# A two-layer spectral kernel on one core: the first transform as a written list over two chunks and three matrices, with weights prepared beside it

## The chip, the core and the metric

The kernel runs on one core of a Trainium2 chip. The metric is the device time of one execution in microseconds. The engines are named as the profile names them: PE (matrix multiplication; PEld is its loading of weights), DVE (vector engine), ACT (scalar engine), POOL (GpSimd) and SP, whose queue issues all DMAs of this kernel.

## The reference

`x` is [4, 256, 256, 64] in float32: batch, rows h, columns w, channels. Layer 0 works on each image, layer 1 along the rows for each channel.

```python
# layer 0
h  = layernorm(x) @ w_te + b_te                        # 64 -> 128 channels
F  = fft2(h, axes=(1, 2))
fc = gelu(concat(real(F), imag(F)) @ w_fc + b_fc)
sp = real(ifft2(fc[..., :128] + 1j * fc[..., 128:], axes=(1, 2)))
x1 = x + sp @ w_tp + b_tp
d  = gelu(depthwise_conv3x3(layernorm(x1) @ w_fe + b_fe))
x2 = x1 + d @ w_fp + b_fp
# layer 1: a moving average over 25 rows, the rest filtered per channel
trend = moving_average(x2, 25)
xs = rfft(x2 - trend, axis=1)[:, :128]
ys = einsum('bmnc,cmk->bknc', xs, w_real + 1j * w_imag)
out = trend + irfft(ys padded, n=256, axis=1)
```

## The kernel before

All sums are in float32. Because the first linear step commutes with the transform, the transform is taken over the 64 input channels, and `w_te` is folded into `w_fc` (`wp`). Layer 1 is linear per channel, so for each of the 64 channels the kernel builds one 256x256 matrix (average, transform, weights and inverse together), stores it in DRAM (`m_d`), and at the end multiplies by it.

The stages of one execution are:

- **Preparation** of the weights in the pool `prep` (lines 193 to 308): some twenty small loads, then `centre`, `w_teg`, `wp`, `w_feg`, the taps `w_dwh`, twenty-four products into `wc_main` and `wc_half`, and the edge terms. It stands ahead of everything else in program order. The pool `prep` is closed before the pool `fwd` of the first transform is opened in the same memory.
- **The first transform**, `forward_h`, in 32 chunks for each image. A chunk `j` is loaded into `xt` (`fl`, lines 371 to 379, three buffers). ACT squares it (`fq`, line 328, one buffer); DVE sums it (`fr`, line 331), sums the squares (`fm`, line 338), and forms the variance (`fR` and `fM`, lines 335 and 342); POOL takes the inverse root (`fp`, line 348) and scales the chunk (`fx`, line 355); DVE forms half sums into `xb`, of which there is one buffer (`fa`, line 392), and quarter sums back into `xt` (`fb`, line 412); POOL forms the sum and the difference of the two row halves (`fh0` and `fh1`, line 417), again into `xb`; PE transforms (`y0` and `y1`, line 423); ACT evicts (`yt0` and `yt1`, line 441), and SP stores to `y_d` (line 454).
- **Layer 1's matrices**, `matrices`: for each channel, `first` on PE and its copy on ACT (lines 1091, 1092 and 1094), `second` on PE (line 1101), `third` on DVE (line 1112) and a store to `m_d` (line 1113). Weights come four channels at a time (line 1087).
- **The spectrum**, `spectral`: groups of columns are read back from `y_d` into `yb` (line 483); the special first column is split into `yr` (line 500); then transform along w (`x`, line 528, and `xs`), the mixing product (`m0`, `m1`, line 552), copies, sums and differences (`gc`, `b`, line 571), GELU (`g`, line 575), a fold on POOL (`p`, line 581), projection (`z`, line 605), a turn (`w`, line 622), and the way back along w (`u` to `uf`, lines 654 to 716).
- **The convolution** and the end of layer 0, then layer 1's products (`layer1`, line 1163).

The four engines PE, DVE, ACT and POOL execute their instructions in program order. Program order is written out by hand: `period(n)` walks a list of names with offsets (`SPECTRUM` while only the first transform and the spectrum run, `FULL` when the convolution runs too), and `do(op, index)` first emits whatever `FOLLOWS` says must come earlier. Ahead of the periods stand S0 = 35 calls of `starting(n, m)`. Each treats one chunk and two matrices, so the first transform of image 0 (32 chunks and three of the next image) and all 64 matrices end together. Then `load_group(0)` and `begin(0)` open the spectrum, and `period(n)` follows from n = 35. The queue of SP is filled by a scheduler. PSUM has eight banks of 128 x 512, handed out in turn.

Of the kernel before, what the change touches and what calls it, by code (L numbers as in the profile page):

```python
# [20 lines left out]
C = 64  # L21
# [108 lines left out]
def conv_seq_kernel(ctx: ExitStack, tc: tile.TileContext, a: dict, tables: bass.AP, out: bass.AP):  # L130
# [29 lines left out]
    nc.sync.dma_start(tab, tables[:, :_L0_END])  # L160
# [31 lines left out]

    with tc.tile_pool(name="prep", bufs=1) as prep:

        def load(shape, name, src):
            t = prep.tile(shape, F32, tag=name, name=name)
            nc.sync.dma_start(t, src)
            return t

        w_te = load([C, HID], "w_te", a["w_te"])  # L200
        g1 = load([C, 1], "g1", column(a["g1"]))
        b1 = load([C, 1], "b1", column(a["b1"]))
        b_te = load([HID, 1], "b_te", column(a["b_te"]))
        nc.sync.dma_start(w_fc, a["w_fc"].rearrange("(k p) n -> p k n", p=P))
        with nc.allow_non_contiguous_dma(reason="a few weights, once"):
            nc.sync.dma_start(b_fc, a["b_fc"].rearrange("(k p) -> p k", p=P))
        nc.sync.dma_start(w_tp, a["w_tp"])
        nc.sync.dma_start(b_tp, row(a["b_tp"]))
        nc.sync.dma_start(w_fp, a["w_fp"])

        centre = prep.tile([P, P], F32, tag="centre", name="centre")
        nc.vector.tensor_scalar(centre, ident, float(C) ** 0.5, None, ALU.mult)
        for lo in (0, C):
            dst = centre[lo : lo + C, lo : lo + C]
            nc.vector.tensor_scalar(dst, dst, -(float(C) ** -0.5), None, ALU.add)


        w_teg = prep.tile([C, HID], F32, tag="w_teg", name="w_teg")  # L220
        nc.vector.tensor_scalar(w_teg, w_te, g1, None, ALU.mult)
        ps = bank("ps_teT")
        nc.tensor.matmul(ps[:, :C], w_teg, centre[:C, :C], start=True, stop=True)
        w_tegT = prep.tile([HID, C], F32, tag="w_tegT", name="w_tegT")
        nc.vector.tensor_copy(w_tegT, ps[:, :C])
        ps = bank("ps_wp")
        for k in range(2):
            nc.tensor.matmul(
                ps[k * C : (k + 1) * C, : 2 * HID], w_tegT, w_fc[:, k, :], start=True, stop=True
            )  # L230
        nc.vector.tensor_copy(wp, ps[:, : 2 * HID])

        ps = bank("ps_dc")
        nc.tensor.matmul(ps[:, 0:1], w_te, b1, start=True, stop=True)
        nc.vector.tensor_scalar(v_dc, ps[:, 0:1], b_te, NPOS, ALU.add, ALU.mult)
        nc.vector.tensor_scalar(nw_tp, w_tp, -1.0, None, ALU.mult)
        nc.vector.tensor_scalar(b_tp, b_tp, 2.0 * NPOS, None, ALU.mult)
        nc.vector.memset(at_dc, 1.0)


        w_fe = prep.tile([P, HID], F32, tag="w_fe", name="w_fe")
        g2 = prep.tile([P, 1], F32, tag="g2", name="g2")
        for par in range(2):
            nc.sync.dma_start(w_fe[par * C : (par + 1) * C], a["w_fe"])
            nc.sync.dma_start(g2[par * C : (par + 1) * C], column(a["g2"]))
        b2 = load([C, 1], "b2", column(a["b2"]))
        b_fe = load([HID, 1], "b_fe", column(a["b_fe"]))
        b_dw = load([HID, 1], "b_dw", column(a["b_dw"]))
        taps = a["w_dw"].rearrange("y x i o -> (y x i) o")
        w_dw = load([9, HID], "w_dw", taps)  # L250
        w_dwb = load(
            [P, 9, HID], "w_dwb", row(taps.rearrange("k o -> (k o)")).to_broadcast([P, 9 * HID])
        )
        b_fe9 = load([9, HID], "b_fe9", row(a["b_fe"]).to_broadcast([9, HID]))
        w_feg = prep.tile([P, HID], F32, tag="w_feg", name="w_feg")
        nc.vector.tensor_scalar(w_feg, w_fe, g2, None, ALU.mult)
        ps = bank("ps_feg")
        nc.tensor.matmul(ps[:, :HID], centre, w_feg, start=True, stop=True)
        nc.vector.tensor_copy(w_feg, ps[:, :HID])


        w_dwh = prep.tile([P, 3, 4, HID], F32, tag="w_dwh", name="w_dwh")
        tap = lambda dy: w_dwb.rearrange("p (y x) o -> p y x o", x=3)[:, dy]
        nc.vector.tensor_copy(w_dwh[:, :, 0], tap(0))
        nc.vector.tensor_copy(w_dwh[:, :, 3], tap(2))
        w_mid = prep.tile([P, 3, HID], F32, tag="w_mid", name="w_mid")
        w_sum = prep.tile([P, 3, HID], F32, tag="w_sum", name="w_sum")
        nc.vector.tensor_scalar(w_mid, tap(1), 0.5, None, ALU.mult)
        nc.vector.tensor_tensor(w_sum, tap(0), tap(2), ALU.add)
        for k, op in ((1, ALU.add), (2, ALU.subtract)):  # L270
            nc.vector.scalar_tensor_tensor(w_dwh[:, :, k], w_sum, 0.5, w_mid, ALU.mult, op)
        for dst, lo, dx in (
            (wc_main[0:C, 0], 0, 1),
            (wc_main[C:P, 0], C, 2),
            (wc_main[0:C, 1], 0, 0),
            (wc_main[C:P, 1], C, 1),
            (wc_half[0:C], 0, 2),
            (wc_half[C:P], C, 0),
        ):
            for k in range(4):  # L280
                nc.vector.tensor_tensor(
                    dst[:, k], w_feg[lo : lo + C], w_dwh[lo : lo + C, dx, k], ALU.mult
                )

        ps = bank("ps_b9")
        nc.tensor.matmul(
            ps[0:9, :HID], b2.to_broadcast([C, 9]), w_fe[0:C], start=True, stop=True
        )
        b9 = prep.tile([9, HID], F32, tag="b9", name="b9")
        nc.vector.tensor_tensor(b9, b_fe9, ps[0:9, :HID], ALU.add)  # L290
        r_edge = prep.tile([9, HID], F32, tag="r_edge", name="r_edge")
        nc.vector.scalar_tensor_tensor(r_edge, b9, -1.0, w_dw, ALU.mult, ALU.mult)
        edge = load([9, 2 * N + 8], "edge", tables[0:9, _L0_END:_L1_START])
        ps = bank("ps_ec")
        nc.tensor.matmul(ps, r_edge, edge[:, 0 : 2 * N], start=True, stop=True)
        nc.vector.tensor_copy(edge_cols.rearrange("p e n -> p (e n)"), ps)
        ps = bank("ps_er")
        nc.tensor.matmul(ps[:, 0:8], r_edge, edge[:, 2 * N :], start=True, stop=True)
        nc.vector.tensor_copy(edge_rows.rearrange("p j e -> p (j e)"), ps[:, 0:8])
        ps = bank("ps_w9")  # L300
        nc.tensor.transpose(ps[:, 0:9], w_dw, ident[0:9, 0:9])
        sum9 = prep.tile([P, 1], F32, tag="sum9", name="sum9")
# [50 lines left out]
    def scale(src, dst, rstd):  # L353
        n = src.shape[1]
        nc.gpsimd.tensor_tensor(dst, src, rstd.unsqueeze(2).to_broadcast([P, n, C]), ALU.mult)


    y_ds, u_ds = {}, {}

# [1006 lines left out]
```

## Time and profile before

| what | value |
|---|---|
| median of 4 executions | 4493.59 us (4487.2 to 4506.36) |
| the profiled execution's own time | 4492.93 us |
| its span | 4491.1 us |
| PE busy | 4357.1 us (97%) |
| DVE busy | 3547.8 us (79%) |
| POOL busy | 2803.4 us (62%) |
| ACT busy | 2505.5 us (56%) |
| first load of a chunk of x issued | 26.71 us after the start of the span |
| first matmul of the first transform | 46.61 us |
| first matmul of the spectrum | 342.34 us |

All views show one execution. A group in the list of costly groups has a busy time, a count and a mean duration; the timeline lists single instructions in order of time with their start and duration in us, and in brackets the idle time of the engine before them and what ended it. In the timeline, a 128x512 matmul in float32 is recorded as two instructions. The table by windows gives the busy time of each engine in a stretch of the span, the granted clock of PE (1.00 is full speed) and the busy share of the DMA engines.

### The profile page before, as it was taken

The numbers are of one execution on the slowest core, as the hardware profiler recorded it, in microseconds if no ns is written. First come the engines' busy times: TensorE is split into PE (matmuls) and PEld (weight loads), VectorE is DVE, ScalarE is ACT, GpSimd is POOL, SyncE is SP. The second block draws the span as 40 slices with busy tenths as digits, with TensorE's granted clock in tenths as the row PEclk, the third lists the DMA queues.
The fourth block names the chain that finished last, engine by engine and source line by source line (L and its number), as shares of the span: only waits on it lengthen the run. The fifth ranks groups of instructions, "written<-read, shape, count | busy, mean of one in ns | idle before, by whom it ended". The sixth has DMA issues, their size and how long they took to land.

```text
span 4491.1 us, 63495 instructions
## 1 busy us (share of the span) xinstructions
PE 4357.1 (97%) x22347; PEld 2220.6 (49%) x22347; DVE 3547.8 (79%) x5451; ACT 2505.5 (56%) x3686; POOL 2803.4 (62%) x1806
## 2 busy tenths in 40 slices
PE   7998999899999999999999999999999999999999
PEld 4553333345555555455555555555555455554444
DVE  6778999899999999999999777777777788862222
ACT  2337888666666666666666666666664334331111
POOL 5888999787777777877777555555554555530000
PEclk9999999999999999999999999999999999999999
DMA  5665555434444444444444343333334332329986
GB/s 172 202 192 162 150 152 153 133 103 135 135 134 135 134 128 141 122 132 132 132 132 118 104 113 94 108 100 95 106 106 142 113 98 90 104 82 336 331 327 257
DMA packets 756581, 655.00 MB, mean 146 GB/s; under 512 B 40141, under 2 KB 649375, under 8 KB 747944
## 3 DMA queue, kind: packets, MB, share of 16 engines
q1 hardware_dynamic: 756264, 650.95, 47.4%
q8 instruction: 178, 2.92, 0.3%
q14 instruction: 139, 1.14, 0.1%
HBM read 364.81 MB, written 286.00 MB: 145 GB/s over the span
## 4 chain that ended last, share of the span: by engine, by line
PE 80%; POOL 7%; DVE 4%; issue 4%; DMA 2%; ACT 1%; SPq 0%; POOLq 0%; DVEq 0%; ACTq 0%
PE ps_h_c L903 19%; PE ps_h_c L922 11%; PE ps_o L1163 9%; PE ps_p L552 8%; PE ps_f_c L978 5%; PE ps_z L605 5%; PE ps_s_c L820 5%; PE ps_u L654 4%; PE ps_x L528 4%; PE ps_y L423 3%; POOL xb L417 3%; PE ps_t_c L857 3%; PE ps_ft_c L999 3%; POOL rstd L348 2%; PE ps_zt L622 2%
## 5 line engine op out<-in xcount | busy, mean ns | idle before, releaser
L581 POOL TENSOR_TENSOR g<-g 128x512 f32<-128x512 f32 (+1 forms) x520 | 738.0, 1432 | 521.5 <-ACT g L575 521.4
L903 PE MATMUL ps_h_c<-td_c,wc_main 128*128 128x512 f32 x2048 | 921.7, 593 | 0.0
L571 DVE TENSOR_TENSOR g<-ps_p,g 128x512 f32<-128x512 f32 x1040 | 692.8, 682 | 32.4 <-ACT g L566 14.4
L575 ACT ACTIVATE g<-g,b_fc 128x1024 f32<-128x1024 f32 (+1 forms) x520 | 586.3, 1147 | 179.9 <-DVE g L571 177.5
L348 POOL TENSOR_TENSOR rstd_c<-var_c,minus_half 128x16 f32<-128x16 f32 x128 | 372.0, 2907 | 466.4 <-DVE var_c L342 456.9
L566 ACT COPY g<-ps_p 128x512 f32<-128x512 f32 (+1 forms) x520 | 302.3, 583 | 457.8 <-PE ps_p L552 439.8
L903 PEld LDWEIGHTS ps_h_c<-td_c,wc_main 128*128 128x128 f32 x2048 | 369.1, 190 | 369.8 <-issue 304.2
L552 PE MATMUL ps_p<-xs,wp 64*128 64x512 f32 (+1 forms) x2080 | 519.5, 604 | 32.7 <-ACT xs L543 32.7
L922 PEld LDWEIGHTS ps_h_c<-td_c,wc_half 64*128 64x128 f32 x4032 | 416.4, 187 | 243.4 <-issue 194.1
L922 PE MATMUL ps_h_c<-td_c,wc_half 64*128 64x128 f32 (+1 forms) x4032 | 514.6, 392 | 3.4 <-POOL td_c L877 3.4
L1163 PE MATMUL ps_o<-xc,mt 128*128 128x512 f32 x1024 | 445.0, 596 | 14.8 <-DMA xc<-x_d 14.8
L348 POOL TENSOR_TENSOR rstd<-var,minus_half 128x16 f32<-128x16 f32 x128 | 373.3, 2916 | 84.9 <-DVE var L342 50.5
L954 DVE TENSOR_TENSOR h_c<-h_c,ps_h_c 128x512 f32<-128x512 f32 x512 | 317.5, 683 | 125.3 <-PE ps_h_c L922 125.2
L971 ACT ACTIVATE h_c<-h_c,b_conv 128x1024 f32<-128x1024 f32 x256 | 280.7, 1145 | 201.3 <-DVE h_c L967 201.3
L1177 DVE TENSOR_SCALAR oc<-ps_o,b_fp 128x512 f32<-128x512 f32 x128 | 96.1, 751 | 361.5 <-PE ps_o L1163 361.5
L417 POOL TENSOR_TENSOR xb<-xt 128x512 f32<-128x512 f32 x256 | 324.5, 1290 | 90.4 <-DVE xt L412 86.0
L947 DVE TENSOR_TENSOR h_c<-h_c,ps_h_c 128x512 f32<-128x512 f32 x256 | 175.7, 686 | 198.6 <-PE ps_h_c L922 194.4
L1163 PEld LDWEIGHTS ps_o<-xc,mt 128*128 128x128 f32 x1024 | 195.0, 191 | 264.1 <-issue 238.4
L528 PEld LDWEIGHTS ps_x<-tab,yb 128*64 128x64 f32 x4064 | 243.1, 139 | 129.8 <-issue 91.5
L605 PE MATMUL ps_z<-g,w_tp 128*64 128x512 f32 x1024 | 281.0, 611 | 22.0 <-POOL g L581 20.5
L1175 ACT ACTIVATE oc<-ps_o,b_fp 128x512 f32<-128x512 f32 x128 | 88.0, 687 | 373.1 <-PE ps_o L1163 258.1
L552 PEld LDWEIGHTS ps_p<-xs,wp 64*128 64x128 f32 x2080 | 195.4, 187 | 194.4 <-issue 121.8
(137 smaller groups left out, 7725.3 us busy)
## 6 DMA issues: line engine op xcount, KB each, us to landing
y_d<-yt SPq DMA_DIRECT2D x256, 256.0 KB, 2.5
yb<-y_d SPq DMA_DIRECT2D x256, 256.0 KB, 3.4
x_c<-in_x_dram SPq DMA_DIRECT2D x128, 512.0 KB, 5.0
u_d<-ut SPq DMA_DIRECT2D x256, 256.0 KB, 4.0
x_d<-st SPq DMA_DIRECT2D x128, 512.0 KB, 4.7
xc<-x_d SPq DMA_DIRECT2D x64, 1024.0 KB, 7.5
out_dram<-oc SPq DMA_DIRECT2D x256, 256.0 KB, 3.1
xt<-in_x_dram SPq DMA_DIRECT2D x504, 128.0 KB, 2.5
```

Source lines behind the costliest of these rows:

```text
L348: nc.gpsimd.tensor_tensor(rstd, var, minus_half.to_broadcast([P, n]), ALU.pow)
L417: nc.gpsimd.tensor_tensor(sums[j][:, i], x0, x1, (ALU.add, ALU.subtract)[i])
L528: nc.tensor.matmul(ps[r * C : (r + 1) * C, j * N + t * P : j * N + (t + 1) * P], blk[:, t, k, r * C : (r + 1) * C], tb[:, t, :], start=Tru ...
L552: nc.tensor.matmul(ps[:, :nf], wp[rows, cols], rhs[rows], start=True, stop=r == 1 or not pr["special"],)
L571: nc.vector.tensor_tensor(gt[:, i], re, gt[:, 1], op)
L575: nc.scalar.activation(g, g, AF.Gelu, bias=b_fc[:, half : half + 1])
L581: nc.gpsimd.tensor_tensor(g[:, 0], g[:, 0], g[:, 1], op)
L605: nc.tensor.matmul(ps[r * C : (r + 1) * C, :nf], w_tp, d[:, :nf], start=True, stop=True)
L903: nc.tensor.matmul(ps, wc_main[:, par, k, :], ts[(*j, k)].rearrange("p j i -> p (j i)"), start=True, stop=False,)
L922: nc.tensor.matmul(pss[k, par][:, s * P : (s + n) * P], wc_half[lo : lo + C, k, :], ts[(*at_q, k)][lo : lo + C, at : at + n, :].rearrange( ...
L954: nc.vector.tensor_tensor(g, g, m, (ALU.add, ALU.subtract)[r])
L1163: nc.tensor.matmul(ps[:, :nf], mts[i // CM][:, i % CM, t, to * P : (to + 1) * P], xc[:, t, :, :, i, :], start=t == 0, stop=t == 1,)
```

## The change

- The preparation becomes a generator, `prepare(prep)`: its loads come first, and its arithmetic is cut into pieces at thirty-two `yield`s, single products of `wc_main` and `wc_half` among them. Two pieces are taken in each call of `starting` from n = 1 on. `prep` gets memory of its own beside `matrices`, on the side of the convolution. The loads of chunk 0, of layer 1's tables and first weights, and of chunk 1 stand ahead of the loads of `tab` and of the weights.
- `starting(n, prep)` now treats two chunks and three matrices, in the order of the list `FIRST`, and is called 17 times. This covers 34 chunks and 51 matrices.
- For the chunks of image 0 (`j < 32`) the difference `fh1` is formed on DVE; the sum `fh0` stays on POOL.
- A matrix is now four names, `v`, `vc`, `mm` and `mt`, which a list can place.
- Between the first transform and the spectrum, four more matrices and the steps of chunk 34 are emitted after `load_group(0)` and ahead of `begin(0)` (`BETWEEN`).
- The last nine matrices go beside the spectrum: the first eleven periods (n = 35 to 45) follow the list `SPECTRUM_AND_MATRIX`. The convolution's pool is opened after them.

The later periods follow the same lists as before. `statistics` and `scale` only move in the file.

```diff
+        yield            # (in prepare: after the loads, and between pieces of the arithmetic)
...
             for k in range(4):
+                yield
                 nc.vector.tensor_tensor(
                     dst[:, k], w_feg[lo : lo + C], w_dwh[lo : lo + C, dx, k], ALU.mult
                 )
...
-            nc.gpsimd.tensor_tensor(sums[j][:, i], x0, x1, (ALU.add, ALU.subtract)[i])
+            engine = nc.vector if i and j < P // 4 else nc.gpsimd
+            engine.tensor_tensor(sums[j][:, i], x0, x1, (ALU.add, ALU.subtract)[i])
...
         def first(c):
-            ps = bank(f"ps_v_{c}")
...
+            if c % CG == 0 and c + CG < C:
+                load(c + CG)
+            ps = pss[c] = bank(f"ps_v_{c}")
...
+        load(0)
+        return {"v": first, "vc": between, "mm": second, "mt": third}
...
+    FIRST = numbered("""
+        v mm:-4 mt:-4 mm:-2 y1:-2 fq fl:1 vc fr yt1:-2 y0:-2 fm fR mm fM v:1 fq:1 fa:-1 v:2 fb:-1 fp
+        fh1:-1 fm:1 fh0:-1 mt:-2 yt0:-2 fr:1 y1:-1 fR:1 y0:-1 fx mt fM:1 fa fb fp:1 fh0 fl:2 fh1
+        fx:1 vc:2 vc:1 yt0:-1 yt1:-1
+    """)
+    SPECTRUM_AND_MATRIX = numbered("""
+        x:1 fq g1:-1 x z:-2 xs:1 zs:-2 v xs fl:1 p1:-1 w:-2 vc b0:-1 fr fm zt:-2 g0:-1 p0:-1 m0 m1
+        gc1 y1:-2 u b1 z:-1 gc0 fx:-1 b0 zs:-1 y0:-2 fR g1 w:-1 us fM yt1:-2 fa:-1 g0 mm:-1 m1:1 uc
+        p1 m0:1 fb:-1 yt0:-2 gc1:1 b1:1 gc0:1 p0 fh1:-1 mt:-1 fp uf fh0:-1 zt:-1
+    """)
...
+    BETWEEN = [
+        numbered("fl:1 fq fr fR"), numbered("fm fM fp"), numbered("fa:-1 fb:-1 fh0:-1 fh1:-1"),
+        numbered("fx y0:-2 y1:-2 yt0:-2 yt1:-2"),
+    ]
+    AHEAD = len(BETWEEN)
+    BESIDE = C - 3 * (S0 // 2) - AHEAD
...
-    def starting(n, m):
-
-        products, add = m
-        rows = lambda text, n: [do(op, n) for op in text.split()]
-        rows("fq", n)
-        rows("fl", n + 1)
-        rows("fr fR fm fM fp", n)
-        rows("fa fb", n - 1)
-        add()
-        products(2 * n)
-        add()
-        if n + 1 < S0:
-            rows("fx", n)
-        rows("y0 y1 yt0 yt1", n - 2)
-        rows("fh0 fh1", n - 1)
-        products(2 * n + 1)
+    def starting(n, prep):
+
+        for i, (op, at) in enumerate(FIRST):
+            do(op, (3 if op in MATRICES else 2) * n + at)
+            if n and i % (len(FIRST) // 2) == 0:
+                next(prep, None)
...
-                for n in range(S0):
-                    starting(n, m)
-                m[1]()
+                do("fl", 1)
+                nc.sync.dma_start(tab, tables[:, :_L0_END])
+                pieces = prepare(prep)
+                next(pieces)
+                nc.sync.dma_start(b_fp, row(a["b_fp"]).to_broadcast([P, C]))
+                for n in range(S0 // 2):
+                    starting(n, pieces)
+                for _ in pieces:
+                    pass
+                do("yt0", FWD - 1)
+                do("yt1", FWD - 1)
                 load_group(0)
+                for k, names in enumerate(BETWEEN):
+                    do("v", C - BESIDE - AHEAD + k)
+                    do("vc", C - BESIDE - AHEAD + k)
+                    do("mt", C - BESIDE - AHEAD + k - 1)
+                    for op, at in names:
+                        do(op, S0 - 1 + at)
                 begin(0)
-            ops |= spectrum
+                ops |= spectrum
+                for n in range(S0, S0 + BESIDE + 2):
+                    period(n)
+                do("mt", C - 1)
             conv = right.enter_context(tc.tile_pool(name="conv", bufs=2, side="right"))
```

## The prediction

> **What bounds the kernel now.** I read the page's forty slices first, for where PE is not full.
>
> ```profile
> span 4491.1 us, 63495 instructions
> PE   7998999899999999999999999999999999999999
> ```
>
> Only slices at the start (112 us each) have room. The change ends at about 500 us; after that the lists are the same, so what is won or lost by then is the answer. Next I read busy time by windows up to 500 us.
>
> ```profile
> 0.00:26.70 26.70, 7.22 (x20) 4.16 (x21) 12.36 (x50) 0.00 (x0) 0.70 (x6) 1.00 0.57 163
> 26.70:60.00 33.30, 26.21 (x70) 12.89 (x70) 20.18 (x29) 9.81 (x15) 19.34 (x10) 0.90 0.42 123
> 60.00:320.00 260.00, 260.00 (x932) 143.95 (x928) 192.33 (x291) 90.52 (x146) 213.62 (x117) 1.00 0.64 200
> 320.00:342.30 22.30, 11.34 (x34) 4.88 (x32) 17.73 (x27) 5.51 (x10) 17.54 (x10) 0.84 0.65 200
> 342.30:400.00 57.70, 51.03 (x308) 23.33 (x310) 45.74 (x69) 41.45 (x64) 47.06 (x32) 0.88 0.55 165
> 400.00:500.00 100.00, 92.91 (x572) 37.12 (x570) 93.25 (x136) 85.65 (x130) 93.91 (x58) 1.00 0.52 148
> ```
>
> The columns are window, length, busy PE, PEld, DVE, ACT and POOL, PE's clock, DMA. PE is full from 60 to 320. It is idle for 19.5 and 7.1 us in the two windows before that, for 11.0 between 320 and 342 and for 6.7 up to 400; after that, in the steady spectrum, PE, DVE and POOL are all at 93% and none has room. Then I read one chunk of the first transform in the timeline.
>
> ```profile
> 201.97 1.94 PE L423 MATMUL ps_y<-xb,tab 128*64 128x512 f32 x8
> 203.84 1.13 PE L1091 MATMUL ps_v<-t,w 128*128 128x512 f32 x2
> 204.03 1.29 DVE L392 TENSOR_TENSOR xb<-xt 128x512 f32<-128x512 f32 x2 [0.67 <-PE ps_y L423]
> 205.36 1.29 DVE L412 TENSOR_TENSOR xt<-xb 128x512 f32<-128x512 f32 x2
> 205.66 1.89 PE L1101 MATMUL ps_m<-t,vs 128*128 128x256 f32 x8
> 208.37 2.50 POOL L417 TENSOR_TENSOR xb<-xt 128x512 f32<-128x512 f32 x2
> ```
>
> `xb` has one buffer, so the next `fa` waits for `y` (0.67 us). One chunk takes 8.95 us (the next `y` starts at 210.93). Last, the start.
>
> ```profile
> 26.46 0.16 DVE L308 TENSOR_TENSOR b_conv<-bp,b_dw 128x1 f32<-128x1 f32 x1
> 26.71 0.37 SPq L374 DMA_DIRECT2D xt<-in_x_dram  x1
> ```
>
> The first load of x is issued when the last preparation ends: `fwd` waits for the memory of `prep`.
>
> **The start.** Chunk 0 now loads at about 0.7 us, 26 earlier; from load to first `y` took 19.9 us (26.71 to 46.61). But DVE's order now has `mt` of matrix 0 ahead of the first `fa`, a wait before had no need of, with var of chunk 1 and everything after queued behind it. Six loads of x at 0.5 us put the tables at 3.9 and the first weights at 4.4 and 4.9; before, these landed 7.6 to 8.2 us after issue, so `v` starts at about 12.5. At the cold rate (25.96 to 29.54) it takes 3.6, the copy 0.6, `mm` 1.8 to 3.4: 20. `mt` 0.7, `fa`, copies, `fb`, `fh1`, `fh0` 4.5, so about 25; on PE a small product waiting for DVE's `w_teg` and one `mm` come first: the first `y` ends at about 30 (bounds 27 and 34; 51.5 before). `tab`, which `y` needs, is issued at about 7 and has landed by then.
>
> **The loop of two chunks.** PE alone, start to start: `v` 1.82 after a transform, else 1.71 to 1.82; `mm` 1.83 ahead of one, else 1.73; `y` 1.87. Three matrices and two chunks: 14.5 us. ACT: squares 2 x 1.06, seven copies of 0.59, 6.3. POOL: 2 x (2.91 + 1.99 + 1.25) = 12.3. DVE: 192.33 in 260 us is 6.62 a chunk, less two `mt` (1.36) is 5.3, plus 0.69 for `fh1`; twice, plus three `mt`, is 14.0. So it looks like a tie of PE and DVE, but `xb`'s ring is longer. From `y` of the odd chunk to `y` of the next even one: 2.06 to `fa`, 1.33, 1.33 to the end of `fb` and its successor's start, then `fh1` 0.69 and `fh0` 1.25, and 0.1 for two hand-overs: 6.76. PE has between them only `y`, `v`, `mm`, 5.52. It waits 1.24 in each period: 15.7 us. This takes `fh1` and `fh0` one after the other, though on two engines. The row for it:
>
> ```profile
> 509.79 3.49 POOL L581 TENSOR_TENSOR g<-g 128x512 f32<-128x512 f32 x2
> 510.91 1.24 DVE L703 SCALAR_TENSOR_TENSOR ut<-ut,ut 128x1024 f32<-128x1024 f32 x1
> ```
>
> Two folds of 1.28 (the group's median) took 3.49 when a DVE operation on two SBUF inputs came between them. If there were no such exclusion, 15.0.
>
> The Trainium skill, "SBUF — State Buffer", section "Who interferes with whom", says that a DVE instruction with two SBUF inputs shuts out a GpSimd instruction that reads SBUF, and the reverse, for the whole instruction. That speaks against splitting `fh0` and `fh1` over these engines; the row above agrees (about 0.9 us lost in 3.49), and by the rule the period is 15.7, without it 15.0.
>
> Even so, per pair of chunks and three matrices it is 15.7 against 14.5 of work, where before PE was full: 16 periods lose about 20 us that the start must pay. From the end of the first `y`: 15 periods, plus 9.0 (`mm`, `mm`, `v`, `v`, `y`) to the last `y` of image 0: 30 + 235.8 + 9 = 275.
>
> **Preparation in pieces.** Its DVE work is 12 us in window one. Two slots a period fall into DVE's 1.7 of slack (15.7 less 14.0), with total, squares and `fa` queued behind them: nothing if POOL is not in a two-input operation, else up to 1.3 or 2. The last piece puts five small matmuls in PE's queue ahead of the last `y`, each waiting for DVE: 2 to 3 us. I take 5 (0 to 12): 280. Before, that `y` ended at 329.2.
>
> **The transition.** PE has four `v`, five `mm` and a `y`: 17.9 us. They cover store, reload (2.8 and 3.4 us to landing) and evictions, about 11. Not covered: the four `yr` products are behind the last `mt` in DVE's order, so the spectrum's first matmul waits for `mm`, `mt` 0.7, `yr` 1.1 to 3.0: 2.5 (1 to 5). It starts at about 300 against 342.3: 42 us earlier, with nine `v` and ten `mm` still owed, 33.7 us of PE.
>
> **Matrices beside the spectrum.** A period is 13.94 us (POOL's scaling at 500.55 and 514.48), with PE waiting 0.84 for `xs` (at 512.7), so 13.1 of work; plus 3.54 it is 16.6, bound by PE. DVE gains 0.68, ACT 0.6, the SP queue one 256 KB store a period and two weight loads every fourth: the second half of `yb` now stands behind a store that waits for `mt`, but is read a period later. Eight steady periods absorb 0.84 each, 6.7; the ramp from 342 to 400, with 6.7 idle, some 4. Owed: 33.7 - 10.7 = 23. The convolution's six first loads of x, spread over 341 to 361 before, now come in one row in SP's queue ahead of `xt` and `yb`: 2 us (0 to 5).
>
> **Sum.** 42 - 23 - 2 = 17 us earlier. The profiled execution took 4492.9 (its span and 1.8 around it; the median is 0.7 higher): 4476.
>
> **Rivals.**
> *No exclusion:* 15.0 a period, 11 us more: 4465. Against it stands the fold's row.
> *Period near 16.7:* pieces of preparation meet POOL's two-input operations and DVE falls late for `fa`. 15 us back: 4490, no difference that counts (0.3%, 13.5 us, is about what a measurement of this kernel can tell from no change).
> *Slower:* the odd chunk's load becomes the ring. Its buffer is free only when `fh0` of two chunks before ends; then 0.1, three issues 1.5, the landing, square 1.06, squares 1.13, two sums and small steps 1.25 + 0.25 + 0.2, three `mt` 1.8, root 2.91, `fh0` 1.25, hand-overs 0.3: 11.7 and the landing. At the 2.5 us of this stage's loads that is 14.2, below 15.7. It decides from a landing of 4.0; each us beyond costs 15 or 16. At 6.5 us the period is 18.2, 4476 + 39 = 4515. For it: the weights landed in 3.4 to 4.2 in that stage and 8 at the start. Against it: DMA engines are busy 0.64 and the bytes per us hardly grow.
>
> **How the numbers follow.** Forecast case (4466 to 4486) 0.55; no exclusion 0.17; near 16.7 0.15; the load's ring 0.13. Unknown costs: exclusion -11, start -3 to +4, preparation -5 to +7, transition and lists beside the spectrum -3 to +9. The range 4461 to 4495 leaves out the load's ring and the ends of the others. Faster by over 0.3% (below 4480): most of the forecast case and all of the second, 0.64; within 0.3%: 0.23; slower 0.13.
>
> **What would show it.** Right: first load near 0.7 us, first transform matmul near 28, `y` pairs every 15.7 with PE idle about 1.2 ahead of the even chunk's, released by POOL's line of `fh0`; the spectrum's first matmul near 300; eleven periods at 16.6. Wrong: PE idle ahead of the odd chunk's `y`, ACT's square waiting for a DMA, or spectrum periods over 17.5.

## The result, and the profile after

The median of the changed kernel is 4489.29 us (33 executions, 4478.72 to 4500.19), that of the kernel before 4493.92 us (53 executions, 4487.2 to 4506.36): a ratio of 0.9990, 95% interval 0.9986 to 0.9995. That is 4.6 us: the interval ends below 1, but the gain is a third of the 0.3% that the prediction set as the least that a measurement can tell. The forecast was 17 us. The profiled execution took 4483.23 us, and its span is 9.6 us below that of before. So there are two questions: why not 17, and why 9.6 in one execution and 4.6 in the middle of many. For the second it helps to know that the times of both kernels spread: their standard deviation is 4.2 us before and 5.1 us after.

The forty slices of the page after first.

```profile
span 4481.5 us, 63463 instructions
PE   7989899799999999999999999999999999999999
```

Slice four (336 to 448 us), at 8 before, is full now, but slice three, full before, is at 8. The table by windows has the same stretches and columns as before.

```profile
0.00:26.70 26.70, 12.29 (x28) 6.08 (x29) 12.60 (x22) 5.05 (x6) 11.93 (x11) 0.96 0.68 197
26.70:60.00 33.30, 29.76 (x99) 16.09 (x98) 23.47 (x42) 10.27 (x17) 19.35 (x9) 0.87 0.56 167
60.00:320.00 260.00, 236.57 (x867) 125.79 (x865) 235.79 (x361) 92.89 (x145) 196.42 (x93) 0.99 0.66 202
320.00:342.30 22.30, 19.98 (x126) 10.77 (x124) 21.02 (x29) 15.24 (x26) 16.70 (x12) 1.00 0.34 107
342.30:400.00 57.70, 56.78 (x323) 26.47 (x320) 48.19 (x69) 44.85 (x69) 46.58 (x29) 1.00 0.40 119
400.00:500.00 100.00, 92.56 (x539) 42.59 (x537) 89.16 (x125) 75.48 (x116) 82.19 (x51) 0.97 0.60 182
```

PE gained 5.1, 3.6, 8.6 and 5.8 us in the first, second, fourth and fifth window. In the third it gave back 23.4 us, while DVE there went from 192 to 236 us. The room at the start is used, and the loop, with the transition that now falls into the same window, pays for it. The timeline of the loop shows how; `fa` is L402, `fb` L422, `fh1` and `fh0` L429, a piece of the preparation L338, the loads of x L384 and L389.

```profile
155.52 1.94 PE L435 MATMUL ps_y<-xb,tab 128*64 128x512 f32 x8
157.57 1.29 DVE L402 TENSOR_TENSOR xb<-xt 128x512 f32<-128x512 f32 x2 [0.27 <-PE ps_y L435]
158.90 1.29 DVE L422 TENSOR_TENSOR xt<-xb 128x512 f32<-128x512 f32 x2
160.23 0.69 DVE L429 TENSOR_TENSOR xb<-xt 128x512 f32<-128x512 f32 x1
160.36 1.69 POOL L429 TENSOR_TENSOR xb<-xt 128x512 f32<-128x512 f32 x1
160.84 1.35 DVE L338 TENSOR_TENSOR wc_main<-w_feg,w_dwh 64x128 f32<-64x128 f32 x1
162.10 1.94 PE L435 MATMUL ps_y<-xb,tab 128*64 128x512 f32 x8 [1.01 <-POOL xb L429]
...
163.52 0.47 SPq L389 DMA_DIRECT2D xt<-in_x_dram  x1
...
167.94 1.06 ACT L210 ACTIVATE sq<-xt 128x1024 f32<-128x1024 f32 x1 [3.96 <-DMA xt<-in_x_dram]
...
169.03 1.22 DVE L220 TENSOR_REDUCE squares<-sq 128x16 f32<-128x1024 f32 x1 [1.01 <-ACT sq L210]
169.31 1.90 POOL L237 TENSOR_TENSOR xt<-xt,rstd 128x1024 f32<-128x1024 f32 x1
170.17 1.18 DVE L338 TENSOR_TENSOR wc_main<-w_feg,w_dwh 64x128 f32<-64x128 f32 x1
...
179.22 1.94 PE L435 MATMUL ps_y<-xb,tab 128*64 128x512 f32 x8 [2.59 <-POOL xb L429]
```

The first seven lines are the ring of `xb` in a regular round (a round is two chunks and three matrices): 6.58 us from the odd chunk's `y` to the even one's, where 6.76 was forecast, and PE idle for 1.01. A regular round takes 15.53. Then comes a long round, 17.12 us. A chunk's load lands late: ACT's square of it starts only 3.95 us after the last issue ended (2.21 in the round that began at 146.57), so `squares` starts 6.93 us after the even `y` and not 5.95 as in that round. The piece behind it in DVE's order now falls into GpSimd's scaling (L237) and takes 1.18 instead of the 0.43 it took there. All that DVE has queued behind them, `fa` of the next even chunk included, and with it `fh0` and `y`, comes 1.6 later: about 1.0 from the load and 0.7 from the piece.

Counted from the first even `y`, the third, ninth and fourteenth rounds are long (17.28, 17.11 and 17.36). The third is long without a late load:

```profile
72.61 1.22 DVE L220 TENSOR_REDUCE squares<-sq 128x16 f32<-128x1024 f32 x1
...
73.86 2.01 POOL L237 TENSOR_TENSOR xt<-xt,rstd 128x1024 f32<-128x1024 f32 x1
74.03 2.25 DVE L324 TENSOR_TENSOR w_sum<-w_dwb 128x384 f32<-128x384 f32 x1
```

Here `squares` waits for nothing, but the piece is a larger one, `w_sum`, and meets the scaling. In the first experiment below (e1), where it does not meet it, the same instruction takes 0.55 (at 73.31, the scaling ended at 73.17).

These marks tell where each run won or lost time. The columns are start of the first `y`, start of the sixteenth even `y` (the last of image 0), the spectrum's first matmul, GpSimd's scaling of chunk 52, and the span, all in us, each from one profiled execution.

| run | first `y` | last even `y` | spectrum | chunk 52 | span |
|---|---|---|---|---|---|
| before | 46.61 | 318.35 | 342.34 | 598.15 | 4491.1 |
| after | 29.64 | 274.25 | 307.53 | 589.00 | 4481.5 |
| after, second profile (e11) | 30.44 | 283.02 | 317.96 | 600.70 | 4496.2 |
| second `xb` (e1) | 29.81 | 271.60 | 306.54 | 589.30 | 4478.5 |
| fourth `xt` (e2) | 29.01 | 271.31 | 304.59 | 587.09 | 4479.9 |
| fourth `xt`, timed (e9) | 28.78 | 270.05 | 303.33 | 586.73 | 4481.3 |
| pieces cut otherwise (e3) | 23.82 | 289.25 | 319.87 | 604.55 | 4497.5 |
| `fh1` on GpSimd (e4) | 24.34 | 285.78 | 320.41 | 602.99 | 4494.4 |
| pieces behind `fa` (e5) | 23.55 | 274.64 | 312.26 | 596.00 | 4492.3 |
| matrices in front (e6) | 28.07 | 282.34 | 349.10 | 602.82 | 4499.9 |
| pieces in front (e7) | 49.81 | 283.39 | 314.01 | 598.87 | 4495.7 |
| rings and pieces (e8) | 26.11 | 271.95 | 302.57 | 583.93 | 4482.9 |
| even rounds (e10) | 27.38 | 255.30 | 286.43 | 573.03 | 4474.4 |

From chunk 52 to the end all of them take 3889 to 3901 us. This spread of 12 us is not the change's, so a difference in spans alone is not read below that. The marks ahead of it differ by up to 12 us between the two profiles of after, which are one program, so the experiments below are read mainly from single rounds. Each of e1 to e8 is one profile. The texts of the expectations also say TensorE for PE and VectorE for DVE.

### The profile page after: what moved, and what is told of

Read it like the earlier page. It is cut to its first block, busy times and chain, and to the rows that moved or that the text cites. A ratio compares the mean times of both kernels' runs of the same rounds, so it can differ in the third digit from the quotient of the medians.

```text
span 4481.5 us, 63463 instructions
## 1 busy us (share of the span) xinstructions
PE 4345.5 (97%) x22347; PEld 2219.1 (50%) x22347; DVE 3585.5 (80%) x5483; ACT 2508.9 (56%) x3686; POOL 2776.3 (62%) x1774
## 4 chain that ended last, share of the span: by engine, by line
PE 83%; DVE 6%; POOL 4%; DMA 3%; ACT 2%; issue 2%; SPq 1%; DVEq 0%; ACTq 0%; POOLq 0%
PE ps_h_c L915 19%; PE ps_h_c L934 11%; PE ps_o L1166 9%; PE ps_p L564 9%; PE ps_f_c L990 5%; PE ps_z L617 5%; PE ps_s_c L832 5%; PE ps_u L666 4%; PE ps_x L540 4%; PE ps_y L435 4%; PE ps_ft_c L1011 3%; PE ps_t_c L869 3%; PE ps_zt L634 2%; DMA xc<-x_d 1%; POOL xb L429 1%
## 5 line engine op out<-in xcount | busy, mean ns | idle before, releaser
L564 PE MATMUL ps_p<-xs,wp 64*128 64x512 f32 (+1 forms) x2080 | 513.8, 601 | 23.3 <-ACT xs L555 23.3
L1166 PE MATMUL ps_o<-xc,mt 128*128 128x512 f32 x1024 | 444.8, 596 | 16.3 <-DMA xc<-x_d 16.3
L230 POOL TENSOR_TENSOR rstd<-var,minus_half 128x16 f32<-128x16 f32 x128 | 382.7, 2990 | 73.4 <-DVE var L224 73.4
L429 POOL TENSOR_TENSOR xb<-xt 128x512 f32<-128x512 f32 x224 | 290.7, 1313 | 97.6 <-DVE xt L422 96.1
```

Source lines behind the costliest of these rows:

```text
L230: nc.gpsimd.tensor_tensor(rstd, var, minus_half.to_broadcast([P, n]), ALU.pow)
L429: engine.tensor_tensor(sums[j][:, i], x0, x1, (ALU.add, ALU.subtract)[i])
L564: nc.tensor.matmul(ps[:, :nf], wp[rows, cols], rhs[rows], start=True, stop=r == 1 or not pr["special"],)
L1166: nc.tensor.matmul(ps[:, :nf], mts[i // CM][:, i % CM, t, to * P : (to + 1) * P], xc[:, t, :, :, i, :], start=t == 0, stop=t == 1,)
```

## The experiments

**What holds the loop: `xb`, x's loads, the place of the pieces, GpSimd.** Four edits of the changed kernel, one thing each (the third takes two).

A second `xb` buffer, for the odd chunks of image 0 (`extra` is a pool beside `prep`):

```diff
-            xb = pool.tile([P, 2, 2, 2, WH, C], F32, tag="xb", name=f"xb_{j}", bufs=1)
+            other = j % 2 and j < NCH
+            xb = (extra["pool"] if other else pool).tile(
+                [P, 2, 2, 2, WH, C], F32, tag="xb", name=f"xb_{j}", bufs=1
+            )
```

> The changed kernel with a second buffer for the half sums xb (odd chunks of image 0 take it from memory beside the matrices). Theory A (the ring through the one xb buffer sets the period of 15.5 us): the waits of about 1.0 us ahead of the even chunk's transform go, regular periods fall to 14.6 to 15.0, some periods of 16 to 17 stay because the odd chunk's load is then the next ring; last transform of image 0 ends 5 to 10 us earlier than 287.7. Rival B (DVE's own work of 14 us, pieces of preparation and its waits for POOL set the period): periods stay at 15.3 or more, the end moves by less than 3 us.

Measured: the rounds behind the first take 14.6 to 16.8, 15.7 in the mean, against 15.9 in the first profile of after. Some now start with PE idle for only 0.15 or not at all, others for 2.0. With the ring gone DVE is idle for only 0.2 to 0.4 us in half of these rounds: its own work, lengthened by the pieces that meet GpSimd (0.29, 0.43 and 1.47 us for the same product in one stretch), is the next bound and holds the round at nearly the same length. The last `y` of image 0 ends at 286.4, 1.4 us earlier than in the first profile of after, as rival B had it (less than 3) and not theory A (5 to 10).

A fourth x buffer, for every fourth chunk:

```diff
-            xt = pool.tile([P, 2, 4, WH, C], F32, tag="xt", name=f"xt_{j}", bufs=3)
+            other = j % 4 == 3 and j < NCH
+            xt = (extra["pool"] if other else pool).tile(
+                [P, 2, 4, WH, C], F32, tag="xt", name=f"xt_{j}", bufs=1 if other else 3
+            )
```

> The changed kernel with a fourth buffer for the loaded chunks xt (every fourth chunk of image 0 takes it from memory beside the matrices). Theory A: the three long periods (17.1 to 17.4 us) come from the load of the odd chunk, which can be issued only when its buffer is free; with the fourth buffer all regular periods are 15.5 and the last transform of image 0 ends about 5 us earlier than 287.7; ACT's squares wait little for DMA (47 us between 60 and 280 before). Rival: the long periods come from pieces of the preparation that meet POOL's two-input operations; then they stay, and the end moves by less than 2 us.

Measured: from the fifth round on every round is 15.52 to 15.54; the long rounds are gone there, and only the third (17.27, with `w_sum` at 2.25 again) and the fourth remain. So the loads' ring makes the later long rounds, and neither the third nor the regular round is touched by it. The last `y` ends 2.9 us earlier, between theory A's 5 and the rival's 2.

The pieces cut otherwise: two products to a piece, and more cuts where PE reads a result of DVE.

```diff
         nc.vector.tensor_scalar(w_teg, w_te, g1, None, ALU.mult)
+        yield
         ps = bank("ps_teT")
...
             for k in range(4):
-                yield
+                if k % 2 == 0:
+                    yield
```

> The changed kernel with the preparation cut elsewhere: a cut ahead of each matmul that reads what DVE has just made, and two products of the convolution's weights in a piece in place of one. Theory A: the first period (21.5 us from the first even transform to the second) loses about 4 us and the last (11.6 us where 8.95 are regular between even and odd transform) about 2.5, so the last transform of image 0 ends about 6 us earlier than 287.7. Rival: these belong to the cold clock and to the loads at the start; then less than 2 us.

Measured: the first `y` starts at 23.82, 5.8 earlier, since PE no longer waits 3.64 us for `w_teg`. But most rounds up to the thirteenth take 17.0 to 17.6, none of them under 15.8. Its timeline has the reason (L341 is the piece there).

```profile
159.13 2.23 DVE L341 TENSOR_TENSOR wc_main<-w_feg,w_dwh 64x128 f32<-64x128 f32 x2
159.26 1.95 POOL L237 TENSOR_TENSOR xt<-xt,rstd 128x1024 f32<-128x1024 f32 x1
```

Two products that take 0.28 each by themselves take 2.23 together when they meet the scaling. From the first `y` to the last even one it takes 265.4 us, where the two profiles of after take 244.6 and 252.6. This is the prediction's rival "period near 16.7" with its own mechanism, brought about by a small edit.

`fh1` back on GpSimd:

```diff
-            engine = nc.vector if i and j < P // 4 else nc.gpsimd
+            engine = nc.gpsimd
```

> The changed kernel with the difference fh1 back on POOL (one part of the change undone). If DVE and POOL excluded each other wholly, the split of fh0 and fh1 would bring only what the shorter DVE operation saves: the ring is then 2.06 + 2.62 + 2.5 + 0.1 = 7.3 against 6.58 measured, so periods of about 16.2, and the last transform 10 us later than 287.7. If POOL's total (14.8 us a period) or its order decides, more: 17 or above.

Measured: from the fifth round on, rounds of 16.34 to 16.36, some of 17.1. A regular round, with `fh0` and `fh1` one after the other on GpSimd, is 0.81 longer than with `fh1` on DVE. So the ring is what the split shortens, by about 12 us in fifteen rounds. From the first `y` to the last even one this run takes 261.4 us.

**Which of a piece's two costs counts.** The pieces are drawn behind `fa`, while GpSimd raises `rstd`.

```diff
-            if n and i % (len(FIRST) // 2) == 0:
+            if n and op == "fa":
                 next(prep, None)
```

> The two pieces of each round are drawn behind fa (VectorE's sum and difference while GpSimd raises rstd) instead of behind fh0 and fh1. Theory 1 (the ring of the one xb buffer sets the round: odd chunk's y, fa, fb, fh1, fh0, even chunk's y): the piece now stands inside the ring, so a round of two chunks grows from 15.53 by a piece's 0.28 to 15.8, and the piece's being shorter on VectorE brings nothing. Theory 2 (pieces that meet GpSimd's scaling and fh0 set it: 0.43 and 1.35 us for one that takes 0.28 when it meets nothing): VectorE has 1.2 us less in a round, the round falls to 15.0 or less. Both: the first y no longer stands behind w_teg's piece (TensorE's 3.64 us wait at 25.3 goes), so it starts at 24 to 26 instead of 29.64. Last y of the first image ends (after: 287.7) at 283 to 288 by theory 1, 275 to 279 by theory 2.

Measured, from its timeline:

```profile
152.28 0.29 DVE L338 TENSOR_TENSOR wc_main<-w_feg,w_dwh 64x128 f32<-64x128 f32 x1
...
161.10 0.28 DVE L338 TENSOR_TENSOR wc_main<-w_feg,w_dwh 64x128 f32<-64x128 f32 x1
...
164.49 1.94 PE L435 MATMUL ps_y<-xb,tab 128*64 128x512 f32 x8 [1.08 <-POOL xb L429]
```

Every product takes 0.27 to 0.29, and still the regular rounds became 15.61 and 15.83 (15.72 in the mean, 0.19 more), as theory 1 had it: what counts in them is the ring, which now has a piece in it. Against that, the long rounds behind the third are gone here too, with three x buffers. So, as far as these runs go, a long round needs a piece that falls into the scaling, and a late load is what moves it there: in e7, which has no pieces in the loop, a load that lands nearly as late (4.02 us after its last issue began, in the fourth round) makes the round 0.26 longer, not 1.6. The first `y` came at 23.55, a little ahead of the 24 to 26 expected, but the first three rounds took 25.3, 19.4 and 17.8, and the last pieces, drawn behind the last `y`, made the stretch from the last even `y` to the spectrum 4.3 longer. At chunk 52 it stands between the two profiles of after.

**Beside the spectrum or in front of it.** All 64 matrices are finished ahead of `begin(0)`.

```diff
-            names = SPECTRUM_AND_MATRIX if n - S0 < BESIDE + 2 else SPECTRUM
+            names = SPECTRUM
...
+                for c in range(C - BESIDE, C):
+                    do("v", c)
+                    do("vc", c)
+                    do("mt", c - 1)
+                do("mt", C - 1)
                 begin(0)
```

> The nine matrices that go beside the spectrum are all made before its first chunk; the spectrum's chunks run without them from the start. The matrices by themselves take at least TensorE's own 33.7 us (nine v, ten mm), so the spectrum's first matmul moves from 307.5 to about 341 or later. Theory 1 (beside the spectrum they cost what the trace of after shows, about 2.03 us a chunk over 9 chunks and the rest at its edges, 25.6 in all): the scaling of chunk 52 on GpSimd comes at 589.0 + 33.7 - 25.6 = 597, 8 us later, and the time is 8 us more. Rival (beside the spectrum they are not hidden at all, 33.7 either way): chunk 52 at 589, no difference. Second rival (in front they also pay the hand-offs TensorE to ScalarE to TensorE and the loads, 0.7 us and more for each): 15 us later.

Measured: this run, the same program as after up to the last `y`, reached its last even `y` 8.1 us later, so only stretches are compared. From the last even `y` to the spectrum's first matmul it took 66.8 us instead of 33.3 in the first profile of after: 33.5 more, PE's own time and no hand-offs. From there to chunk 52 it took 253.7 instead of 281.5: 27.8 less. Beside the spectrum the nine matrices are therefore hidden by only 5.7 of 33.5 us. Against the second profile of after (34.9 and 282.7) it is 2.8 of 31.8. So little of them is hidden, the rival with hand-offs (15) is out, and between the first theory (8) and the first rival (0) one profile does not decide.

**What cutting the preparation up is worth.** All pieces ahead of the first chunk:

```diff
-                next(pieces)
+                for _ in pieces:
+                    pass
```

> All pieces of the weights' preparation are done before the first chunk instead of two in a round. VectorE then waits for the weights' loads (the last is issued at 20.5) before it may reduce the first chunk, and has some 13 us of its own and TensorE's work in the pieces: first y at about 50 instead of 29.64. Theory 1 (the xb ring sets the regular round, pieces lie beside it): rounds stay 15.5, the first round loses its extra 6 us, the last y its 2.7 us: the last y of the first image ends 8 to 14 us later than 287.7. Theory 2 (the pieces set the round): rounds fall to 15.0 or less and the three long ones go as well, which gives back 8 + 5 more: about even.

Measured: its first `y`.

```profile
49.81 1.94 PE L435 MATMUL ps_y<-xb,tab 128*64 128x512 f32 x8 [0.44 <-POOL xb L429]
```

The first `y` starts 20.2 us later, and the loop without pieces gives most of it back: all fifteen rounds take 15.53 to 15.83, 233.6 us in all against 244.6 (first profile of after), and the tail from the last even `y` to the spectrum 30.6 against 33.3. At the spectrum it is 6.5 us behind the first profile of after, a little less than theory 1's 8 to 14, and 4.0 ahead of the second. Loop and tail are thus 13.7 us shorter than in one execution of after and 23.3 shorter than in the other. Of this, 6.0 in each are the first round (15.5 here, 21.5 there), and they are not the pieces' alone: PE's granted clock over that round is 1.00 here and 0.90 there.

**All of it together.** Both buffers of e1 and e2, the pieces behind `fa` (two for the odd chunk), and the cuts of e3 without its pairs.

```diff
-            if n and i % (len(FIRST) // 2) == 0:
+            if n and op == "fa":
                 next(prep, None)
+                if at < 0:
+                    next(prep, None)
```

> A second xb buffer for odd chunks, a fourth xt buffer for every fourth chunk, the pieces behind fa (one for the even chunk, two for the odd one) and cut so that no piece has VectorE's result read by TensorE in the same piece. If xb's ring, the loads' ring and the pieces that meet GpSimd are together what holds the round above TensorE's 14.5: rounds of 14.5 to 15.0, first y at about 24, last y of the first image ends at 255 to 262 (after: 287.7), the spectrum's first matmul at about 280, chunk 52's scaling at 561 to 568, time 4455 to 4463. If VectorE's own work holds the round (the run with a second xb buffer alone had 15.7): rounds of 15.3 to 15.7, last y ends at 268 to 275, time 4466 to 4474.

Measured: eight rounds in the middle take 14.6 to 14.9, near PE's 14.5. DVE is idle for only 0.14 to 0.23 us in them, so the two are about tied, and the ring and the loads count for little. But the loop ended at neither expectation. The first round takes 23.2 us, and the second, twelfth and thirteenth take 19.4, these three for one reason; the twelfth in the timeline (L416 is `fa`, L346 a small product of the preparation, L436 `fb`):

```profile
204.47 1.30 DVE L416 TENSOR_TENSOR xb<-xt 128x512 f32<-128x512 f32 x2
...
209.74 0.38 PE L346 MATMUL ps_b<-w_fe,b 64*9 64x128 f32 x2
...
210.16 0.27 DVE L351 TENSOR_TENSOR b<-b_fe,ps_b 9x128 f32<-9x128 f32 x1 [4.39 <-PE ps_b L346]
...
210.68 1.27 DVE L436 TENSOR_TENSOR xt<-xb 128x512 f32<-128x512 f32 x2
```

A piece that both issues a product on PE and reads it on DVE makes DVE wait until PE's queue has come to it, here 4.39 us, with `fb` and so the next `y` behind it. The next version draws the product and its reading in different pieces, puts three products of the weights in a piece, and loads chunk 2 ahead of the weights.

```diff
         nc.tensor.matmul(ps[:, :HID], centre, w_feg, start=True, stop=True)
+        yield
         nc.vector.tensor_copy(w_feg, ps[:, :HID])
...
                 nc.sync.dma_start(tab, tables[:, :_L0_END])
+                do("fl", 2)
```

> As the run with both rings and the pieces behind fa, and besides: a piece's matmul and VectorE's copy of it are drawn in different pieces (there VectorE waited 4.1 to 4.8 us for TensorE in five half rounds, and those rounds took 19.4), three products of the weights go in one piece, and chunk 2's load is issued ahead of the weights' loads. If these waits were what was left: first y at 25, the first round 16 to 18 instead of 23, the other rounds 14.7 to 15.2, the last even y of the loop at 248 to 256 (after: 274.25), the spectrum's first matmul at 279 to 286 (after: 307.5), the median 4460 to 4468. If VectorE's waits only move elsewhere (the banks that the pieces hold longer, the loads of the first rounds): last even y at 262 to 272, median 4474 to 4484.

Measured: median 4469.66 us (5 executions, 4465.47 to 4476.15) against 4497.98 for the kernel before on the same chip, a ratio of 0.9934, 95% interval 0.9920 to 0.9947. It beats both kernels: its slowest execution is below the fastest of after (4478.72). The first `y` came at 27.4, later than the 25 expected. The first round takes 17.1, the second 16.8, the others 14.5 to 15.5; the last even `y` came within the first expectation, the spectrum and the median 0.4 and 1.7 us above it. Its table by windows for the middle of the loop:

```profile
60.00:260.00 200.00, 196.69 (x715) 104.58 (x714) 195.89 (x325) 74.71 (x118) 175.63 (x81) 1.00 0.71 219
```

PE is busy for 98% and DVE as well: the tie of the two that the prediction had named ahead of the ring. The run takes several steps at once, so what each is worth by itself is not shown.

**Why the median gained less than the profile.** The fourth x buffer again, timed, and the changed kernel itself a second time.

> The fourth x buffer again, now timed. The first transform's loop of after is the same program in two profiles and took 274.25 in one and 282.34 in the other to its last even y: the rounds that are longer than 15.53 (three and eight of them) come and go with the landing of x's loads. Theory 1 (this is why the median of after is only 4.6 below that of before while the profiled execution is 9.6 below): with the fourth buffer the long rounds are gone from the fifth round on in every execution, and the median falls from 4489.3 to 4480 to 4485, 9 to 14 below the kernel before. Rival (the spread comes from the later stages, which this does not touch): the median stays at 4487 to 4491 and the single profile's 3 us is all that is seen of it there.

> The changed kernel itself, profiled and timed a second time. Theory 1 (the long rounds of the loop come and go from execution to execution with the landing of x's loads, three in the first profile, more in the loop of the run with the matrices in front): the number of rounds over 16.5 between the second and the sixteenth even y differs again from three, and the scaling of chunk 52 stands off 589.0 by 1.3 to 1.8 for each; the ratio to the kernel before is again 0.9985 to 0.9995. Rival (the loop of after is always the one of its first profile, and the matrices in front lengthened it by changed addresses): three long rounds again, at the same places, chunk 52 at 588 to 590, and the spread of its times arises behind chunk 52.

Measured for e9: median 4487.15 (11 executions) against 4497.98 for the kernel before on the same chip, ratio 0.9977, 95% interval 0.9968 to 0.9986. The 10.8 us are within the 9 to 14 of theory 1; the median in itself is within the rival's 4487 to 4491, but on that chip the kernel before took 4 us more as well. The interval touches that of after (0.9986 to 0.9995) at its end, so a gain by the fourth buffer is likely and its size open. The spread did not shrink (standard deviation 4.4 us). Measured for e11: median 4494.99 (11 executions) against 4498.54, ratio 0.9992, 95% interval 0.9983 to 1.0001, and a loop with seven rounds above 16.5 instead of three. These are PE's even `y` at two of them:

```profile
85.13 1.94 PE L435 MATMUL ps_y<-xb,tab 128*64 128x512 f32 x8 [2.73 <-POOL xb L429]
...
182.84 3.44 PE L435 MATMUL ps_y<-xb,tab 128*64 128x512 f32 x8 [2.59 <-POOL xb L429]
```

The last even `y` came 8.8 us later than in the first profile, chunk 52 11.7 later (theory 1 gives 5 to 7 for four more long rounds; the rest is a first `y` 0.8 later, two slow `y`, and 2.9 behind the last even `y`), and the span was 14.7 longer: it is 5.1 above the span of before, where the first was 9.6 below. The long rounds stand at the places where the first profile has them, and a second and third one follow there. So the loop of after itself differs by some 8 us between executions, and the first profile is one of its good ones. In the profile of before all rounds behind the first take 17.90 or 17.91: it shows nothing of the kind. Yet the times of before spread by 4.2 us too, and e9 without the later long rounds by 4.4. The spread as a whole is therefore not the long rounds', and how much of the step from 9.6 to 4.6 they explain is not shown: part of it may be only that the profiled execution of after is 6.1 us below its median and that of before 1.0.

## Why the prediction was right or wrong

The time fell into the range, but the likeliest case, faster by 17 us, did not come; the result is the case "within 0.3%". That the range holds is the width of it and not its sum. The median is also the 4490 of the rival "period near 16.7". Its mechanism, pieces that meet GpSimd's two-input operations, is in the long rounds, and the mean of all fifteen rounds is 16.3 and 16.8 in the two profiles; but the regular round is 15.53, and the rest comes from the first round and the late loads, so the agreement of the number is in part luck. Point by point:

- **The start.** First load at 0.73 us, right. The first `y` ended at 32.55, not 30: `w_teg` took 1.85 us beside GpSimd's scaling, and the first `y` itself took 2.91 (1.94 in the loop), at a granted clock of 0.66 over these 2.91 us.
- **The ring of `xb`.** Right: PE waits for GpSimd's `fh0` ahead of each even `y`, 1.01 (1.24 forecast), and a regular round takes 15.53 (15.7). Without any pieces it is 15.53 as well (e7). The Trainium skill, "SBUF — State Buffer", "Who interferes with whom", has GpSimd's reads shut out for the whole of a DVE operation with two SBUF inputs. Here `fh0` began 0.13 after `fh1` and took 1.69 instead of 1.27: the two take 1.82 together, 1.96 strictly one after the other. The rule holds to 0.14 us here, and the rival without exclusion falls with this row. For GpSimd's power it does not hold (the last section), and there the measurement decides.
- **Preparation in pieces.** This is the step that failed. The sum without it put the last `y`'s end at 274.8 and allowed 5 us (0 to 12) for the pieces. It ended at 287.8, 13.0 later: the first `y` 2.5; the fifteen rounds, from end to end of their `y`, 7.8 (6.0 more in the first: PE is busy for 3.4 us more, by the pieces' products and a clock of 0.90, and idle for 2.5 more, as `ps_feg` holds it for 3.54 until DVE's `w_feg`, behind a wait of DVE of 3.09 for PE's `ps_wp`; 5.6 more in the four longest of the others; 2.8 less in the sum of all by the shorter ring; 1.0 less since the long first `y` is already counted); and the last piece's five products 2.6, as forecast. Against e7, loop and tail are longer by 13.7 in this execution and by 23.3 in the other, and neither is within the term's 0 to 12. The forecast counted a piece's own length and up to 2 us where it meets GpSimd; it let DVE's slack of 1.7 take that up. It did not count that a late load of x moves a piece into the scaling, nor that PE and DVE wait for one another where a piece has a product on PE and its reading on DVE.
- **The load ring.** It was set down as a rival that decides from a landing of 4.0 us, and put aside because the stage's loads land in 2.5. That was taken as one number for all rounds. In the ninth round of after it was 3.95 to 4.4 (to ACT's square, from the end of the last issue, or its start) and in the next one under 3. In the fourteenth the landing was as usual, but the last issue itself took 1.47 instead of 0.47. So late loads made two of fifteen rounds long in the first profile, not all or none; in the second they made three, and three more are long right behind these. A late load alone costs little (e7, 0.26): the ring of the loads is not the bound by itself. With the fourth buffer these rounds are regular (e2, e9), and the third is 17.27 and 17.28 still. The prediction's sign for this case, ACT's square waiting for a DMA, does not tell it: it waits so in regular rounds too (1.67 at 160.44).
- **The transition.** Right: 19.7 us from the last `y`'s end to the spectrum's first matmul, 20.4 forecast. That matmul came at 307.53 and not 300 because the loop ended late: 34.8 us earlier than before instead of 42.
- **Matrices beside the spectrum.** Right in size: from that matmul to chunk 52 it takes 281.5 us, before 255.8, so 25.7 with the convolution's loads (23 + 2 forecast); a period beside the spectrum takes 15.97 (16.6), so more than forecast is lost at the edges. e6 has nearly the same cost, 27.8 against the first profile and 29.0 against the second.
- **The sum.** 34.8 - 25.7 = 9.1 at chunk 52, and 9.6 in the span, where 42 - 25 = 17 was forecast. In the second profile it is 24.4 - 26.9 = -2.5. The median's 4.6 lies between the two.
- **The reading of the slices.** "Only slices at the start have room" is not quite so: slice eight (786 to 898 us) stands at 8 as well. The change does not reach it.

Two things stay open. What makes a load of x come late in one round and not in the next is not shown: the loads of layer 1's weights are issued near some of the long rounds and not near others. And the 12 us of spread behind chunk 52, where the programs are alike, have no cause shown here.

## What to carry to other kernels

Work put into the gaps of a loop is priced by what stands behind it in its engine's order: here 0.28 us of a product became 1.2 to 2.0 us beside GpSimd, and one reading of a product just issued on PE 4.4 us of everything behind it. Put such pieces where the other engine runs an operation that doesn't shut them out, and draw a product and its reading at different places. When two rings are within 10% of each other (15.5 and 14.2 here), a landing time that varies by 1.5 us can decide between them anew in each round. The spare buffer belongs to the ring whose time varies: a fourth x buffer made the rounds even, a second `xb` alone did not. And one profile is not enough to judge by.

## What the runs showed of the hardware that was not expected

- GpSimd's power of 128x16 (`rstd`) lets DVE's sums and differences through at full speed: a product beside it took 0.27 to 0.29 us in e5, the same as in before and in e7, where GpSimd is idle beside it (0.28 to 0.29). The power itself took 2.91 where it began first, and 3.28 to 3.39 where a sum was running as it began. Beside GpSimd's scaling of 128x1024 the order of the two decides: a product that began up to 0.25 ahead of it took 0.27 to 0.43, one that began 0.02 to 0.87 behind it 1.18 to 2.03 (after, e1, e6, e11). So a delay of some 0.2 us makes a short piece a long one. The rows of the power are from after:

```profile
141.98 2.91 POOL L230 TENSOR_TENSOR rstd<-var,minus_half 128x16 f32<-128x16 f32 x1 [1.65 <-DVE var L224]
142.05 1.29 DVE L402 TENSOR_TENSOR xb<-xt 128x512 f32<-128x512 f32 x2
...
149.25 1.30 DVE L402 TENSOR_TENSOR xb<-xt 128x512 f32<-128x512 f32 x2
149.41 3.29 POOL L230 TENSOR_TENSOR rstd<-var,minus_half 128x16 f32<-128x16 f32 x1 [0.98 <-DVE var L224]
```

- After a wait of the same 2.59 us, `y` took 1.94 in one execution (after, 179.22) and 3.44 in another (e11, 182.84), where the granted clock over the next 3.5 us was 1.00 and 0.56. A long round can so cost another 1.5 us, in two of the seven of e11. In e8 a wait of 2.24 us was enough (241.38: 3.56 at a clock of 0.52).
